# Four edits around the scan of a four-layer model: residual, softplus buffers, order of the state sums, and a shorter beginning

## The chip, the cores and the metric

The kernel runs on one core of a Trainium2 chip. The metric is the device time of one execution in microseconds (us), lower is better. The engines are named as in the profile: PE (TensorE, the matmuls; PEld are its weight loads), DVE (VectorE), ACT (ScalarE), POOL (GpSimd) and SP (SyncE, here a queue of DMAs). Each engine runs its own list of instructions in order, and waits where an instruction needs something that another engine or a DMA has not finished. Everything is float32.

## The reference, cut to what matters

The model takes `x` of 32 sequences, 256 positions each, 128 features. It has four layers of two halves. In front of each half there is a layer norm whose scale and shift depend on the sequence, and behind it a residual with a gate that depends on the sequence too:

```
mod = silu(c) @ wmod                     # one set of six vectors per layer
sa, ca, ga, sb, cb, gb = mod[:, 0..5]
ga, gb = (2*(g>=0) - 1) * max(|g|, 0.25) # for each of the two gates
h = layernorm(x) * (1 + ca) + sa
x = x + ga * attn(h)
h = layernorm(x) * (1 + cb) + sb
x = x + gb * ffn(h)
```

The change touches the setting up of `mod`, the reading of `x`, and the first half of the first layer, a selective scan (two branches, each with a softplus for `u` and one for `delta`):

```
xn    = layernorm(h);  xp = xn @ proj.T + b;  z = silu(xp)
u     = softplus(xp @ conv_br.T + b_br)
delta = softplus((u @ dbc[:, :64].T) @ dt.T + dt_b);  B, C = u @ dbc[:, 64:].T
state[t] = exp(delta[t] * A) * state[t-1] + delta[t] * B[t] * u[t]     # 16 states per feature
y_br[t]  = sum_n C[t, n] * state[t, n] + D * u[t]
out   = (y_0 + y_1) * z + h
```

The other seven halves (two mixtures of experts with capacity or dense, two attentions of other kinds, a linear attention, a mixture by heads and an MLP with FP4 rounding) are the same before and after.

## The kernel before, in words

The tokens are kept in SBUF for the whole kernel as 16 tiles `x[b]` of 128 features by 512 tokens (two sequences each). `run` calls `begin` and then the eight halves one after the other; each opens its own pools of buffers, so a half begins when the buffers of the one before are free.

**The beginning** (`begin`, L602 to L634). One DMA on ACT's queue brings `cT` and `wmod` of all four layers (`mw`, 1600 KB). For each layer there is a sigmoid (`sigmoid`, L552 to L556), six matmuls of 128 by 32, and some twenty tiny operations on DVE and ACT. For each of the 16 tiles there is a DMA of 256 KB (`xin`, three buffers, ACT's and SP's queue in turn), four transpositions on PE, and a copy to `x[b]`, on DVE or ACT in turn.

**The scan** (`scan_layer`). The work is written out as an agenda of steps: `put(t, f)` records that `f` is issued in step `t`, and within a step in the order of the calls. Tile `b` starts at step T = 16 b. The pair p = 8 b + 4 br + g takes two steps, `scan_even` in 2p and `scan_odd` in 2p + 1; one pair is four of the sixteen states of one branch:

- `scan_even`: 16 matmuls fill `dB` (four PSUM banks, one buffer), then DVE runs four scans `hs<-decay,dB` (L849) that read it. Then `scan_turned`: PE transposes half of the `hs` of the pair before into `hT` (one buffer of two banks), ACT copies it to `hsT0`. Then `scan_decay`: ACT makes two `decay` arrays for the next pair. Then `scan_weigh`: eight matmuls add the half `hsT1` of p - 2 into the state sums `y` (one PSUM bank, one buffer).
- `scan_odd`: `scan_turned` for the other half (`hsT1`), `scan_weigh` of `hsT0` of p - 1, `scan_decay`.

Between these lie the parts that prepare the tiles to come, and they all share a single PSUM bank, `tp` (the transposition bank): the two layer norms (steps T - 44 to T - 32), `scan_proj` (T - 21), the gate (T - 20, T - 19), `scan_u` and `scan_u2` (softplus of u, T - 19 and T - 18; T - 13 and T - 12 for the second branch), `scan_delta` and `scan_rows` (softplus of delta and the rows B and C, T - 15 and T - 14; T - 7 and T - 6), `scan_turn`, `scan_b`, `scan_c`. Behind the last pair of a tile ACT copies the sums (`scan_sum`, `yT`, T + 18), PE turns them back (`scan_end`, T + 21), DVE adds `uu` (L908), POOL multiplies by `z` and adds `h` (L914, L915), and in T + 23 DVE adds the residual into `x[b]` (L533).

A softplus is in two parts: `soft_start` (DVE, L739 and L740: `sp_r` = max(v + bias, 0), `sp_m` = v - 2 `sp_r`; one buffer each) and `soft_end` (ACT: exp and log on `sp_m`; POOL, L746: the sum of `sp_m` and `sp_r` into `u` or `dl`).

**What sets the order.** PE's matmuls and ACT's activations in the scan go through `mm`, `tr` and `act` (L386, L390, L393), which keep them in the order of the program. DVE's and POOL's instructions here don't: where they stand in their engine's list is decided when the kernel is built, by a planner that orders instructions by its own idea of when each could run.

Of the kernel before, what the change touches and what calls it, by code (L numbers as in the profile page):

```python
# [25 lines left out]
ALU = mybir.AluOpType  # L26
# [4 lines left out]
P = 128  # L31
NSEQ, SEQ = 32, 256
NB = 16
# [142 lines left out]
def packs(d):  # L176

    out = {}
# [3 lines left out]
        return g  # L182

    k = Pack()
    k.add("cT", np.stack([np.asarray(d[f"L{n}_c"]).T for n in range(4)], 1))
    k.add("wmod", np.stack([np.asarray(d[f"L{n}_wmod"]) for n in range(4)], 1))
    out["mod"] = k

    g, k = layer(0, "attn"), Pack()
# [120 lines left out]
class Program:  # L310
# [289 lines left out]


    def begin(self):  # L602
        nc, tc = self.nc, self.tc
        nc.scalar.preload_act_table_set(LN_EXP)
        with ExitStack() as ctx:
            self.pools(ctx, {"tp": 4, "mod": 2}, xin=3, mw=1)
            mw = self.wk("mw", (P, self.at["mod"]["n"]))
            nc.scalar.dma_start(mw, self.aps["mod"])
            v = View(mw, self.at["mod"]["at"])
            for n in range(4):  # L610
                sg = self.wk("sg", (P, NSEQ))
                self.sigmoid(sg, v.cT[:, n, :])
                nc.vector.tensor_tensor(sg, sg, v.cT[:, n, :], ALU.mult)
                ps = self.ps("mod", (P, 6, NSEQ))
                for j in range(6):
                    nc.tensor.matmul(ps[:, j, :], v.wmod[:, n, j * P : (j + 1) * P], sg, start=True, stop=True)
                m = self.mods[:, n]
                for j in (0, 3):
                    nc.scalar.copy(m[:, j, :], ps[:, j, :])
                    nc.vector.tensor_scalar(m[:, j + 1, :], ps[:, j + 1, :], 1.0, None, ALU.add)  # L620
                    neg, mag = self.wk("neg", (P, NSEQ)), self.wk("mag", (P, NSEQ))
                    nc.vector.tensor_scalar(neg, ps[:, j + 2, :], -1.0, None, ALU.mult)
                    nc.vector.tensor_tensor(mag, ps[:, j + 2, :], neg, ALU.max)
                    nc.vector.tensor_scalar(mag, mag, 0.25, 2.0, ALU.max, ALU.mult)
                    nc.vector.tensor_scalar(neg, ps[:, j + 2, :], 0.0, 0.5, ALU.is_ge, ALU.subtract)
                    nc.vector.tensor_tensor(m[:, j + 2, :], neg, mag, ALU.mult)
            xd = self.aps["x"].rearrange("(b t p) f -> b p t f", p=P, t=4)
            for b in range(NB):
                xi = self.wk("xin", (P, 4, P))
                (nc.sync if b % 2 else nc.scalar).dma_start(xi, xd[b])  # L630
                ps = self.ps("tp", (P, 4, P))
                for t in range(4):
                    nc.tensor.transpose(ps[:, t, :], xi[:, t, :], self.c.ident)
                (nc.scalar.copy if b % 2 else nc.vector.tensor_copy)(self.x[b], ps.rearrange("p a b -> p (a b)"))  # L634


    def scan_layer(self, w):

        nc = self.nc
        with ExitStack() as ctx:
            self.pools(
                ctx, {"dB": 1, "hT": 1, "y": 1, "tp": 1},
                h=4, z=3, dl=3, duT=3, bc=3, xn=1, ln_xn=1, xp=1, y=1, yT=1, rows=1, Xc=1, du=1, sg=1, hsT0=1, hsT1=1, sp_m=1, sp_r=1, Xr=1,
            )
# [8 lines left out]
            nc.scalar.copy(wd, pw[:, :P])  # L658
            decay = []
            for n in range(10):  # L660
                t = self.wk_pool.tile([P, 2, SEQ], F, name=f"decay{n}", bufs=1)
                nc.gpsimd.memset(t[:, :, 0:1], 0.0)
                decay.append(t)
            far = ctx.enter_context(self.tc.tile_pool(name="far", bufs=2, space=DRAM))
            s = {"far": far, "w": w, "A": A, "wd": wd, "decay": decay, "p": {}}
            agenda = {}

            def put(t, f, *args):
                agenda.setdefault(t, []).append((f, args))

            for p in range(-1, 8 * NB + 3):
                put(2 * p, self.scan_even, s, p)
                put(2 * p + 1, self.scan_odd, s, p)
            for b in range(NB):
                a = s[b] = {"b": b}
                T = 16 * b
                put(T, self.clear_regions)


                for o, n, src in ((T - 44, 1, lambda a: self.x[a["b"]]), (T - 36, 2, lambda a: a["h"])):  # L680
                    put(o, lambda a, n=n, src=src: a.update({("st", n): self.norm_rows(src(a), self.nc.gpsimd)}), a)
                    put(o + 1, lambda a, n=n: self.scan_roots(a, n), a)
                    put(o + 3, lambda a, n=n: self.norm_scale(a["st", n][0], *a["r", n]), a)
                put(T - 40, self.scan_norm_out, a)
                put(T - 32, self.scan_norm_out2, s, a)
                put(T - 21, self.scan_proj, s, a)
                put(T - 20, self.scan_gate, s, a)
                put(T - 19, self.scan_gate2, s, a)
                for br in (0, 1):
                    o = T + 8 * br  # L690
                    put(T - 19 + 6 * br, self.scan_u, s, a, br)
                    put(T - 18 + 6 * br, self.scan_u2, s, a, br)
                    put(o - 15, self.scan_delta, s, a, br)
                    put(o - 14, self.scan_rows, s, a, br)
                    put(o - 10, self.scan_turn, s, a, br)
                    put(o - 9, self.scan_b, s, a, br)
                    put(o - 5, self.scan_c, s, a, br)
                put(T + 18, self.scan_sum, s, a)
                put(T + 21, self.scan_end, s, a)
                put(T + 23, lambda a: self.residual(0, 0, a["b"], a["y"]), a)  # L700
            for t in sorted(agenda):
                for f, args in agenda[t]:
                    f(*args)
            self.strict = self.strict_act = False

    def scan_roots(self, a, n):
# [26 lines left out]
        self.act(a["z"], a["sg"], AF.Exp)  # L733
        self.nc.gpsimd.tensor_tensor(a["z"], a["z"], a["xp"], ALU.mult)

    def soft_start(self, src, bias):

        m, r = self.wk("sp_m"), self.wk("sp_r")
        self.nc.vector.tensor_scalar(r, src, bias, 0.0, ALU.add, ALU.max)  # L739
        self.nc.vector.scalar_tensor_tensor(m, r, -2.0, src, ALU.mult, ALU.add)  # L740
        return m, r, bias

    def soft_end(self, out, m, r, bias):
        self.act(m, m, AF.Exp, bias=bias)
        self.act(m, m, AF.Ln, bias=1.0)
        self.nc.gpsimd.tensor_tensor(out, m, r, ALU.add)  # L746

    def scan_u(self, s, a, br):
        w = s["w"]
        pu = self.ps("tp")  # L750
        self.mm(pu, w.conv[:, br, :], a["xp"])
        a["soft"] = self.soft_start(pu, w.vec[:, 3 + br : 4 + br])

    def scan_u2(self, s, a, br):
        a["u", br] = self.wk("u")
        self.soft_end(a["u", br], *a["soft"])

    def scan_delta(self, s, a, br):
        pt = self.ps("tp")
        self.mm(pt, s["wd"], a["u", br])  # L760
        a["soft"] = self.soft_start(pt, s["w"].vec[:, 5:6])

    def by_chunk(self, t):

# [2 lines left out]
    def scan_rows(self, s, a, br):  # L767
# [13 lines left out]
        dl = a["dl", br] = self.wk("dl")  # L781
        self.soft_end(dl, *a["soft"])
# [47 lines left out]
    def scan_even(self, s, p):  # L830
# [18 lines left out]
                nc.vector.tensor_tensor_scan(hs[:, :, n], decay, dB[:, :, n], 0.0, ALU.mult, ALU.add)  # L849
        self.scan_turned(s, p - 1, 0)  # L850
        self.scan_decay(s, p + 1, 0)
        self.scan_weigh(s, p - 2, 1)

    def scan_odd(self, s, p):
        self.scan_turned(s, p - 1, 1)
        self.scan_weigh(s, p - 1, 0)
        self.scan_decay(s, p + 1, 1)

    def scan_decay(self, s, p, half):
# [19 lines left out]
    def scan_weigh(self, s, p, h):  # L879
# [1920 lines left out]
```

## Time and profile before

| | us |
|---|---|
| runs | 6774.54, 6795.66, 6796.21; median 6795.66 |
| profiled execution | 6771.9, of which the span is 6769.9 |
| beginning, up to the first matmul of the scan layer | 0 to 43.65 |
| first layer's filling, up to the first `dB` | 43.65 to 125.1 |
| scans | 127.5 to 1100 |
| last residual of the scan | 1107.9 |
| the other seven halves | to 6769.9 |

A line of the timeline gives the start, the duration, the engine, the line of the source, the operation, what it writes and reads, the shape, and how many like it are merged; in brackets stands how long the engine was idle before and what ended that. In the table by stretches each engine has its busy time in that stretch with the number of its instructions; PEclk is the share of full speed that PE's clock was granted. Matmuls of a group overlap, so that the start of the next group is a better mark than the end that is shown. An instruction may be counted in several records (eight matmuls of `y` are 16 records).

### The profile page before, as it was taken

To read this page: it belongs to the slowest core of one execution; us is meant where nothing else is said; L and a number is where in the kernel's file an instruction comes from. 1 tells how busy PE (TensorE), PEld (TensorE's weight loads), DVE (VectorE), ACT (ScalarE), POOL (GpSimd) and SP (SyncE) were. 2 spreads that over 40 slices of the span, in tenths; PEclk is the share of its full clock that TensorE was granted. 3 is DMA by queue.
4 is the path that set the end of the run, shared out by engine and by line. 5 is a ranking of instruction groups with operands and counts; after the bars stand their busy time and mean duration, and the time that the engine had idled before them with its cause. 6 is when DMAs were issued, how large, how long until landed. Compare 5 with 4: busy or idle time off the path is not lost. (4 is left out here: it accounts for less than half of the span.)

```text
span 6769.9 us, 132928 instructions
## 1 busy us (share of the span) xinstructions
PE 5927.9 (88%) x54369; PEld 3341.0 (49%) x54369; DVE 4278.6 (63%) x9929; ACT 3493.9 (52%) x5035; POOL 2650.5 (39%) x2882
## 2 busy tenths in 40 slices
PE   5888886999899999999999767999889998999987
PEld 3555554466455555555566434555422222444444
DVE  3777776611455555555565644777777775677779
ACT  4888884333344444444444322443468886545542
POOL 3555553565444444444444443434234543000000
PEclk6999997999899999999999877888989998999998
DMA  1110111144000000000000101111134442000010
GB/s 60 41 41 29 41 41 35 42 124 119 15 6 5 5 8 5 5 8 5 5 2 2 47 17 26 26 24 26 31 79 90 92 91 49 16 18 18 18 33 30
DMA packets 175445, 232.19 MB, mean 34 GB/s; under 512 B 46519, under 2 KB 95919, under 8 KB 174450
## 3 DMA queue, kind: packets, MB, share of 16 engines
q1 hardware_dynamic: 120656, 124.40, 7.2%
q0 software_dynamic: 26992, 56.62, 3.5%
q10 hardware_dynamic: 27186, 42.67, 1.7%
q8 instruction: 426, 6.98, 0.4%
q14 instruction: 185, 1.52, 0.1%
HBM read 88.22 MB, written 74.97 MB: 24 GB/s over the span
## 5 line engine op out<-in xcount | busy, mean ns | idle before, releaser
L1418 ACT ACTIVATE E<-S 128x1024 f32<-128x1024 f32 x448 | 458.6, 1024 | 602.6 <-PE S L386 535.5
L298 DVE TENSOR_REDUCE mt<-S 128x4 f32<-128x1024 f32 (+1 forms) x512 | 549.8, 1087 | 252.5 <-PE S L386 196.1
L849 DVE TENSOR_TENSOR_SCAN hs<-decay,dB 128x512 f32<-128x512 f32 x512 | 583.0, 1204 | 91.8 <-PE dB L386 77.2
L386 PE MATMUL S<-qa,kx 32*128 32x256 f32 x4096 | 566.8, 396 | 59.8 <-DVE mt L298 39.0
L393 ACT ACTIVATE hid<-S,bigw 128x1024 f32<-128x1024 f32 x512 | 537.2, 1111 | 122.6 <-PE S L386 121.9
L1887 DVE TENSOR_TENSOR E<-S,cst 128x1024 f32<-128x1024 f32 x320 | 391.2, 1223 | 307.3 <-PE S L386 270.7
L1890 POOL TENSOR_SCALAR_AFFINE_SELECT E<-E 128x1024 f32<-128x1024 f32 x320 | 349.3, 1092 | 588.2 <-ACT E L1889 587.9
L386 PE MATMUL S<-kx,q 32*128 32x512 f32 (+1 forms) x2048 | 549.1, 631 | 16.9 <-ACT kx L1536 16.1
L1889 ACT COPY E<-S 128x1024 f32<-128x1024 f32 x320 | 323.5, 1011 | 328.4 <-PE S L386 244.7
L2439 POOL TENSOR_TENSOR acc<-acc,ye 128x512 f32<-128x512 f32 x256 | 344.5, 1346 | 362.7 <-DVE ye L298 319.6
L386 PEld LDWEIGHTS S<-qa,kx 32*128 32x128 f32 x4096 | 360.2, 200 | 178.4 <-DVE mt L298 107.1
L1719 DVE TENSOR_REDUCE mt<-S 128x4 f32<-128x512 f32 (+1 forms) x256 | 205.2, 823 | 320.9 <-PE S L386 312.4
L386 PE MATMUL S<-qG,f 32*128 32x512 f32 x2560 | 382.6, 658 | 4.5 <-DVE E L1887 3.4
L386 PE MATMUL S<-hm,bigw 32*128 32x512 f32 x2048 | 337.3, 650 | 24.8 <-ACT hid L393 24.8
L393 ACT ACTIVATE hsT<-hT 128x1024 f32<-128x1024 f32 x256 | 260.7, 1018 | 157.3 <-PE hT L390 156.2
L393 ACT ACTIVATE decay<-dl,A 128x510 f32<-128x510 f32 x512 | 339.1, 714 | 0.0
L386 PE MATMUL po<-E,vzl 128*32 128x128 f32 x8192 | 286.8, 281 | 59.6 <-POOL E L1890 59.3
L390 PE MATMUL hT<-cst,hs 128*128 128x128 f32 x2048 | 295.9, 290 | 22.6 <-ACT hsT L393 21.4
L386 PE MATMUL po<-hid,bigw 128*32 128x512 f32 x2048 | 279.9, 619 | 31.0 <-DVE ye L298 31.0
L386 PE MATMUL po<-E,vz 128*32 128x256 f32 x4096 | 304.7, 383 | 0.3 <-ACT oc L1438 0.2
L1422 POOL TENSOR_SCALAR_AFFINE_SELECT E<-E 128x512 f32<-128x512 f32 (+1 forms) x192 | 157.7, 822 | 364.4 <-ACT E L1418 363.9
L1766 ACT ACTIVATE E<-S 128x768 f32<-128x768 f32 (+1 forms) x192 | 168.9, 880 | 239.4 <-PE S L386 239.4
(524 smaller groups left out, 13192.1 us busy)
## 6 DMA issues: line engine op xcount, KB each, us to landing
gb<-gT SPq DMA_DIRECT2D x256, 256.0 KB
regions<-zeros ACTq DMA_DIRECT2D x16, 2048.0 KB
rx<-far SPq DMA_DIRECT2D x64, 256.0 KB
expert_rows<-eo SPq DMA_DIRECT2D x39, 256.0 KB
out<-out SPq DMA_DIRECT2D x16, 256.0 KB
xTd<-xT SPq DMA_DIRECT2D x15, 256.0 KB
xT<-xTd SPq DMA_DIRECT2D x15, 256.0 KB
bigw<-in_s SPq DMA_DIRECT2D x10, 256.0 KB
```

Of the source, the lines that this page charges most:

```text
L298: return lambda *args, **kw: self.tc.keep_in_program_order(op(*args, **kw))
L386: return self.tc.keep_in_program_order(self.nc.tensor.matmul(out, lhsT, rhs, start=start, stop=stop, **kw))
L390: return self.tc.keep_in_program_order(self.nc.tensor.transpose(out, in_, self.c.ident[:k, :k]))
L393: ins = self.nc.scalar.activation(*args, **kw)
L849: nc.vector.tensor_tensor_scan(hs[:, :, n], decay, dB[:, :, n], 0.0, ALU.mult, ALU.add)
L1418: nc.scalar.activation(e, src, AF.Exp, scale=scale)
L1719: nc.vector.tensor_reduce(m.rearrange("p (g j) -> p g j", j=2), pm[:, :, x] if i == 0 else pm[:, :, :, 0:192], AX.X, ALU.max, negate=True,)
L1766: nc.scalar.activation(e, src, AF.Exp, scale=1.0 / math.sqrt(8))
L1887: nc.vector.tensor_tensor(e, src, self.c.caus.unsqueeze(1).to_broadcast([P, 8, P]), ALU.mult)
L1889: nc.scalar.copy(e, src)
L1890: nc.gpsimd.affine_select(e, e, [[0, 8], [1, P]], ALU.is_ge, 0.0, base=0, channel_multiplier=-1)
L2439: nc.gpsimd.tensor_tensor(a["acc"], a["acc"], ye, ALU.add)
```

## The change

1. **Beginning.** `begin` now sets up `mod` for layer 0 alone and reads tile 0 alone. The host packs `c` and `wmod` of a layer side by side, so that a layer is one DMA of 400 KB. The other 15 tiles are read and turned in the agenda of the scan: tile b is loaded in step 2b - 47 and turned in step 2b - 45 (into the bank `dB`, which is idle until step 0), all loads on SP's queue with two buffers, all copies on DVE. The layers 1 to 3 of `mod` are loaded in step 8n - 52 and computed in step 8n - 46 (into the bank `y`). These matmuls and transpositions now go through `mm` and `tr`, so that they have a fixed place in PE's list.
2. **State sums.** `scan_weigh` is taken out of `scan_even` and `scan_odd`, and called at the end of the step, behind everything else that the step issues. `scan_sum` follows the last `scan_weigh` of a tile at once, which puts it behind the other parts of step T + 18.
3. **Softplus.** `soft_start` writes its first result straight into `u` or `dl`, and `soft_end` adds in place; `sp_r` is gone, `sp_m` has two buffers instead of one.
4. **Residual.** It is issued in step T + 25 instead of T + 23.

```diff
-            self.pools(ctx, {"tp": 4, "mod": 2}, xin=3, mw=1)
-            mw = self.wk("mw", (P, self.at["mod"]["n"]))
-            nc.scalar.dma_start(mw, self.aps["mod"])
...
+            self.pools(ctx, {"tp": 4, "mod": 2}, xin=3, mw=2)
+            for n in (0,) if some else range(4):
+                self.mod_layer(n, self.mod_load(n), self.ps("mod", (P, 6, NSEQ)))
+            for b in (0,) if some else range(NB):
+                self.turn_in(b, self.load_in(b), self.ps("tp", (P, 4, P)))
+    def mod_load(self, n):
+        mw = self.wk("mw", (P, NSEQ + 6 * P))
+        self.nc.scalar.dma_start(mw, self.aps["mod"][:, n * (NSEQ + 6 * P) : (n + 1) * (NSEQ + 6 * P)])
+        return mw
+    def mod_layer(self, n, mw, ps):
...
+        for j in range(6):
+            self.mm(ps[:, j, :], mw[:, NSEQ + j * P : NSEQ + (j + 1) * P], sg)
...
+    def load_in(self, b):
+        xi = self.wk("xin", (P, 4, P))
+        self.nc.sync.dma_start(xi, self.aps["x"].rearrange("(b t p) f -> b p t f", p=P, t=4)[b])
+        return xi
+    def turn_in(self, b, xi, ps):
+        for t in range(4):
+            self.tr(ps[:, t, :], xi[:, t, :])
+        self.nc.vector.tensor_copy(self.x[b], ps.rearrange("p a b -> p (a b)"))

     def scan_layer(self, w):
...
+            for b in range(1, NB):
+                put(2 * b - 47, lambda b=b: s.update({("xi", b): self.load_in(b)}))
+                put(2 * b - 45, lambda b=b: self.turn_in(b, s["xi", b], self.ps("dB", (P, 4, P))))
+            for n in (1, 2, 3):
+                put(8 * n - 52, lambda n=n: s.update({("mw", n): self.mod_load(n)}))
+                put(8 * n - 46, lambda n=n: self.mod_layer(n, s["mw", n], self.ps("y", (P, 6, NSEQ))))
+            sums = {}
             for p in range(-1, 8 * NB + 3):
...
+                sums[2 * p], sums[2 * p + 1] = (p - 2, 1), (p - 1, 0)
...
-                put(T + 18, self.scan_sum, s, a)
                 put(T + 21, self.scan_end, s, a)
-                put(T + 23, lambda a: self.residual(0, 0, a["b"], a["y"]), a)
+                put(T + 25, lambda a: self.residual(0, 0, a["b"], a["y"]), a)
             for t in sorted(agenda):
                 for f, args in agenda[t]:
                     f(*args)
+                if t in sums:
+                    self.scan_weigh(s, *sums[t])
...
-    def soft_start(self, src, bias):
-        m, r = self.wk("sp_m"), self.wk("sp_r")
-        self.nc.vector.tensor_scalar(r, src, bias, 0.0, ALU.add, ALU.max)
-        self.nc.vector.scalar_tensor_tensor(m, r, -2.0, src, ALU.mult, ALU.add)
-        return m, r, bias
+    def soft_start(self, out, src, bias):
+        m = self.wk("sp_m")
+        self.nc.vector.tensor_scalar(out, src, bias, 0.0, ALU.add, ALU.max)
+        self.nc.vector.scalar_tensor_tensor(m, out, -2.0, src, ALU.mult, ALU.add)
+        return out, m, bias
...
-        self.nc.gpsimd.tensor_tensor(out, m, r, ALU.add)
+        self.nc.gpsimd.tensor_tensor(out, m, out, ALU.add)
...
     def scan_even(self, s, p):
...
         self.scan_decay(s, p + 1, 0)
-        self.scan_weigh(s, p - 2, 1)
     def scan_odd(self, s, p):
         self.scan_turned(s, p - 1, 1)
-        self.scan_weigh(s, p - 1, 0)
         self.scan_decay(s, p + 1, 1)
...
     def scan_weigh(self, s, p, h):
...
+        if p % 8 == 7 and h == 1:
+            self.scan_sum(s, a)
```

More of the change, by code (lines that the diff above doesn't have):

```diff
@@ L184, in packs @@
     k = Pack()
-    k.add("cT", np.stack([np.asarray(d[f"L{n}_c"]).T for n in range(4)], 1))
-    k.add("wmod", np.stack([np.asarray(d[f"L{n}_wmod"]) for n in range(4)], 1))
+    k.add("mod", np.stack([np.concatenate([np.asarray(d[f"L{n}_c"]).T, np.asarray(d[f"L{n}_wmod"])], 1) for n in range(4)], 1))
     out["mod"] = k
@@ L602, in begin @@
     def begin(self):
-        nc, tc = self.nc, self.tc
-        nc.scalar.preload_act_table_set(LN_EXP)
+        self.nc.scalar.preload_act_table_set(LN_EXP)
+        some = 0 in self.stages
         with ExitStack() as ctx:
-            self.pools(ctx, {"tp": 4, "mod": 2}, xin=3, mw=1)
-            mw = self.wk("mw", (P, self.at["mod"]["n"]))
-            nc.scalar.dma_start(mw, self.aps["mod"])
[L609 to L634, printed above, removed]
@@ new lines, in mod_layer @@
+    def mod_layer(self, n, mw, ps):
+        nc = self.nc
+        sg = self.wk("msg", (P, NSEQ))
+        self.sigmoid(sg, mw[:, :NSEQ])
+        nc.vector.tensor_tensor(sg, sg, mw[:, :NSEQ], ALU.mult)
+        for j in range(6):
+            self.mm(ps[:, j, :], mw[:, NSEQ + j * P : NSEQ + (j + 1) * P], sg)
+        m = self.mods[:, n]
+        for j in (0, 3):
+            nc.scalar.copy(m[:, j, :], ps[:, j, :])
+            nc.vector.tensor_scalar(m[:, j + 1, :], ps[:, j + 1, :], 1.0, None, ALU.add)
+            neg, mag = self.wk("neg", (P, NSEQ)), self.wk("mag", (P, NSEQ))
+            nc.vector.tensor_scalar(neg, ps[:, j + 2, :], -1.0, None, ALU.mult)
+            nc.vector.tensor_tensor(mag, ps[:, j + 2, :], neg, ALU.max)
+            nc.vector.tensor_scalar(mag, mag, 0.25, 2.0, ALU.max, ALU.mult)
+            nc.vector.tensor_scalar(neg, ps[:, j + 2, :], 0.0, 0.5, ALU.is_ge, ALU.subtract)
+            nc.vector.tensor_tensor(m[:, j + 2, :], neg, mag, ALU.mult)
@@ L647, in scan_layer @@
                 ctx, {"dB": 1, "hT": 1, "y": 1, "tp": 1},
-                h=4, z=3, dl=3, duT=3, bc=3, xn=1, ln_xn=1, xp=1, y=1, yT=1, rows=1, Xc=1, du=1, sg=1, hsT0=1, hsT1=1, sp_m=1, sp_r=1, Xr=1,
+                h=4, z=3, dl=3, duT=3, bc=3, xn=1, ln_xn=1, xp=1, y=1, yT=1, rows=1, Xc=1, du=1, sg=1, hsT0=1, hsT1=1, Xr=1, mw=1,
             )
@@ L734, in scan_gate2, with soft_end @@
         self.nc.gpsimd.tensor_tensor(a["z"], a["z"], a["xp"], ALU.mult)
-    def soft_start(self, src, bias):
-        m, r = self.wk("sp_m"), self.wk("sp_r")
-        self.nc.vector.tensor_scalar(r, src, bias, 0.0, ALU.add, ALU.max)
-        self.nc.vector.scalar_tensor_tensor(m, r, -2.0, src, ALU.mult, ALU.add)
-        return m, r, bias
-    def soft_end(self, out, m, r, bias):
+    def soft_start(self, out, src, bias):
[3 more added lines that the diff above has]
+        return out, m, bias
+    def soft_end(self, out, m, bias):
         self.act(m, m, AF.Exp, bias=bias)
         self.act(m, m, AF.Ln, bias=1.0)
-        self.nc.gpsimd.tensor_tensor(out, m, r, ALU.add)
+        self.nc.gpsimd.tensor_tensor(out, m, out, ALU.add)
     def scan_u(self, s, a, br):
@@ L751, in scan_u @@
         self.mm(pu, w.conv[:, br, :], a["xp"])
-        a["soft"] = self.soft_start(pu, w.vec[:, 3 + br : 4 + br])
+        a["u", br] = self.wk("u")
+        a["soft"] = self.soft_start(a["u", br], pu, w.vec[:, 3 + br : 4 + br])
     def scan_u2(self, s, a, br):
-        a["u", br] = self.wk("u")
-        self.soft_end(a["u", br], *a["soft"])
+        self.soft_end(*a["soft"])
     def scan_delta(self, s, a, br):
@@ L760, in scan_delta @@
         self.mm(pt, s["wd"], a["u", br])
-        a["soft"] = self.soft_start(pt, s["w"].vec[:, 5:6])
+        a["dl", br] = self.wk("dl")
+        a["soft"] = self.soft_start(a["dl", br], pt, s["w"].vec[:, 5:6])
     def by_chunk(self, t):
@@ L780, in scan_rows @@
         nc.gpsimd.tensor_copy(a["Xc"].rearrange("k g r n -> k g n r"), Xc.rearrange("k (g n) r -> k g n r", g=4))
-        dl = a["dl", br] = self.wk("dl")
-        self.soft_end(dl, *a["soft"])
+        dl = a["dl", br]
+        self.soft_end(*a["soft"])
         a["du"] = self.wk("du", (P, 4, 4, 32))
```

## The prediction

> **What bounds the kernel now.** I read the page first (no engine is full, PE 88%, DVE 63%), then the table by stretches, then the timelines of one tile on each engine; the chain that ended last only covers the last thousand microseconds, so it says nothing here. The change touches the first 1108 us. In the table by stretches the filling (43 to 125 us) and the scans (125 to 1100 us) look like this:
>
> ```profile
> 43.00:125.00 82.00, 37.70 (x86) 15.21 (x86) 15.48 (x61) 35.16 (x75) 31.97 (x72) 0.50 0.01 2
> 125.00:1100.00 975.00, 791.25 (x11043) 562.84 (x11042) 726.50 (x897) 795.42 (x1286) 534.44 (x624) 0.94 0.11 40
> ```
>
> In both no engine is full (PE 791 and ACT 795 of 975 us): the time is in chains from engine to engine. The timeline of the beginning:
>
> ```profile
> 9.46 0.29 DVE L552 SCALAR_TENSOR_TENSOR sg_a<-mw 128x32 f32<-128x32 f32 x2 [9.46 <-DMA mw<-in_mod]
> ...
> 20.75 1.09 PE L633 MATMUL tp<-cst,xin 128*128 128x128 f32 x4 [1.24 <-DMA xin<-in_x]
> ...
> 44.80 1.11 PE L390 MATMUL tp<-cst,x 128*128 128x128 f32 x4 [0.36 <-ACT wd L658]
> ```
>
> The beginning waits for transfers; the first layer norm starts at 44.80. The load that PE waits for at 20.75 was issued at 17.69, so a tile's load takes 3 us. DVE in one tile of the scan:
>
> ```profile
> 573.07 0.75 DVE L739 TENSOR_SCALAR sp_r<-tp,w 128x512 f32<-128x512 f32 x1 [2.17 <-POOL dl L746]
> ...
> 580.03 0.65 DVE L908 TENSOR_TENSOR y<-uu,tp 128x512 f32<-128x512 f32 x1
> 584.53 1.32 DVE L533 SCALAR_TENSOR_TENSOR x<-y,mods,x 128x256 f32<-128x256 f32 x2 [3.85 <-POOL y L915]
> 585.77 4.54 DVE L849 TENSOR_TENSOR_SCAN hs<-decay,dB 128x512 f32<-128x512 f32 x4
> 592.60 4.55 DVE L849 TENSOR_TENSOR_SCAN hs<-decay,dB 128x512 f32<-128x512 f32 x4 [2.28 <-PE dB L386]
> ```
>
> A tile takes 62.04 us (585.77 to 647.81, the same four scans of the next tile). Two waits per tile belong to the edits: 3.85 us of the residual for POOL, 2.17 us of `sp_r` for POOL. PE in two places of the same tile, and ACT in the second:
>
> ```profile
> 602.95 0.64 PE L386 MATMUL y<-hsT,Cd 128*32 128x128 f32 x16
> 603.52 1.13 PE L386 MATMUL tp<-xn,w 128*128 128x512 f32 x2
> 604.58 1.17 PE L386 MATMUL dB<-Bd,duT 32*128 32x128 f32 x32
> ...
> 631.96 0.64 PE L386 MATMUL y<-hsT,Cd 128*32 128x128 f32 x16 [0.44 <-ACT yT L393]
> 632.53 1.12 PE L386 MATMUL tp<-xp,w 128*128 128x512 f32 x2
> 633.59 1.17 PE L386 MATMUL dB<-Bd,duT 32*128 32x128 f32 x32
> ```
>
> ```profile
> 631.32 0.58 ACT L393 ACTIVATE yT<-y 128x512 f32<-128x512 f32 x1
> 631.80 0.57 ACT L393 ACTIVATE rows<-tp 32x512 f32<-32x512 f32 x1
> 632.28 0.70 ACT L393 ACTIVATE sp_m<-sp_m,w 128x512 f32<-128x512 f32 x1
> 633.01 0.63 ACT L393 ACTIVATE sp_m<-sp_m 128x512 f32<-128x512 f32 x1
> ```
>
> What to see: `dB` to scan is 1.31 us at least (604.58 to 605.89), a scan group 4.55, and in five of the eight pairs of a tile `dB` starts when PE gets to it, not when DVE frees its bank (598.39, 604.58, 612.86, 626.88, 633.59). There PE comes from a user of `tp`, which had waited for ACT to empty that bank; the eight `y` matmuls (0.57 us) ran during that waiting.
>
> **The residual: 0.** The built program has another order than the agenda suggests. In its list for DVE the residual still stands behind `y<-uu,tp` and ahead of the next four scans, in all 16 tiles: the planner moved it back. So the 3.85 us stay. Had it gone behind the scans, a tile would win at most the wait and its own 1.3 us less what PE needs for `dB`, about 4 us.
>
> **Beginning: -31.6.** By the table in stretches of 2 us, the DMAs had moved 0.66 MB at 4 us, 1.46 at 6, 2.38 at 8. The new beginning needs `mw` of one layer (0.41 MB, alone on ACT's queue) and constants, weights and tile 0 (1.6 MB). By equal shares the bytes of `mw` are through at 4.4 us, those of tile 0 at 7.2. A load of 256 KB takes 3 us, of which 0.6 are bytes at 460 GB/s (the stretch 6 to 8 us); I add half of the rest, 1.2: 5.6 and 8.4. From `mw` (9.46) to the first `mod` matmul (15.7) before, less 3 us in which DVE stood at a copy of `x`, gives 8.7 now; six matmuls and some 15 tiny operations end near 12 us. The scan's pool waits for them, on all queues: the next loads on SP, and `tp<-w` on PE. So the first layer norm starts at about 13.2 instead of 44.80. Bounds: 11 (no wait for the pool) and 16 (transfers as slow as in 20 to 43 us, 127 GB/s, behind the first).
>
> **Filling: +11.7.** What left the beginning is now in PE's list between the steps of the norms: 15 tiles of four transpositions (1.09 us each, the row of 20.75) and 18 small matmuls (six in 1.3 us: twelve took 2.60 to 2.74). Where PE sat idle for 5 us (three `ln_xn`, ACT and POOL at work) two tiles fit in for nothing. In the gaps of about 1 us they don't: two tiles and a layer of `mod` (3.5) stand ahead of `tp<-h`, ahead of the second tile's `tp<-x` and ahead of `proj`, each +2.4 to 2.6; two single tiles +0.4 and +0.2. To this come 2.1 us where ACT has to do the sigmoid of layer 1 before `ln_t`, and that sigmoid waits for the load of `mw` and tile 1 (issued at 12, there at 15 or 16), and 0.8 twice, where eight tiny DVE operations (0.1 us apart) stand between the four `ln_st`. Sum 11.7. With two buffers a load starts when PE has turned the tile two before; by the walk it is there 1 to 5 us ahead of its place. On SP all 15 loads stand ahead of the first `far` (90.46), with nothing else between; the three `mw` loads on ACT's queue wait for nothing late; the 15 copies (0.69) lie in DVE's idle 66 of 82 us. Bounds: 4 (all hidden but the sigmoid and one `mod`) and 22 (15 tiles and three `mod` end to end, 20.3, and the sigmoid).
>
> The Trainium skill ("TensorE: Matmul & The Clock Gate", the HAM clock gate) has PE at half clock until about 3.4 us of sustained work. The row above has 0.50 for the whole filling with PE busy 46% of it. By the page the added work could reach full clock if it closed the gaps; then four transpositions would cost 0.66 as at 574.67, and the filling some 5 us less.
>
> **Softplus and state sums: +1.35 per tile.** I walk one tile in the new order of PE and ACT, with the durations above; scans start before at 592.60, 599.88, 605.89, 614.43, 620.34, 628.38, 636.56 and 647.81. `y` now stands behind the user of `tp`, right ahead of `dB`. ACT's lists are unchanged but for `yT`, so a user of `tp` isn't freed earlier. First pair: no change (PE idle 4.28 before it). Second: `tp<-u,wd` at 597.36 (behind ACT's `h`), `y` 598.39, `dB` 598.96 instead of 598.39, scans 600.27 (+0.39; they waited for `sp_m` before). Third: the pair of hand-overs starts 0.57 late, `tp<-xn,w` again behind ACT's `rows`, `dB` 605.65, scans 606.96 (+1.07). Fourth: ACT was busy without a gap here, so its delay stays 0.57; `dB` 614.00, scans 615.31 (+0.88, `sg` and `sp_m` in between had slack). Fifth: scans end 619.86, but `y` ends at 620.3; scans 621.61 (+1.27). Sixth: ACT's `xn` is 1.2 late, `y` 0.57: `dB` 628.65, scans 629.96 (+1.58). Seventh: the old wait of 2.17 is gone, as `sp_m` has a second buffer and `u` was last read by POOL in the tile before; but `yT` now stands behind `rows` and two `sp_m` on ACT, ends at 635.4 and holds back the first `y` of the next tile, and `dB` behind it: 636.05 instead of 633.59, scans 637.36 (+0.80). Eighth: ACT's `ln_xn` ends 642.3, `tp<-yT` 642.4, DVE's `y` 643.4, residual 647.93, scans 649.16 instead of 647.81: +1.35. So the softplus wins (alone it would give 1.1: the end of the wait moves the scans by 1.46, and ACT's `ln_xn` then sets the rest) and the sums lose more. Bounds per tile: -1.1 (`y` hidden everywhere) and +2.9 (five times 0.57, nothing won). Some 14 tiles have this pattern; the last two have little on `tp`. 14 x 1.35 = +19. The cover: POOL (534 of 975 us busy) delivers `dl` and `du` 2.7 us later, as its `Cd` waits for the last `y`; PE needs `du` 8 us on, so this costs nothing unless POOL falls behind by that.
>
> **Sum.** -31.6 + 11.7 + 19 = -1, against the profiled execution 6771.9. The median of the runs is 6795.66, 24 above it; I carry the change over to the median: 6795. The runs of before lie 22 us apart, about 0.3%, which is also what a measurement can tell from no change.
>
> **The rivals.** Faster, by hidden sums: if ACT's chain and not PE's order sets the five `dB`, as ACT's 82% would allow, a tile gives -1.1 and the sum is -20 - 15 = -35: 6761. Against it: each of the five `dB` follows a matmul within 0.05 us. Faster still: the residual does move in time because POOL's `y` is early; -4 x 14 more, 6740. Against: the order of the list, and POOL's three operations of 1.27 us behind DVE's `y` are unchanged. Slower, by the wait for `yT`: PE now stands still for ACT with `dB` behind it. From 2.5 us per tile on it outweighs the beginning by over 0.3% if the filling also takes its upper half: 14 x 2.9 = 41, less 31.6, plus 16: +25, 6821. For it: `y` waited 0.44 for `yT` even before. Last, the moved work is no gain at all (filling 22), with the tile as walked: +9, still no change that can be told.
>
> **How the numbers follow.** Chances: forecast (within 20 us) 0.45; hidden sums 0.27; residual moved 0.03; `yT` and sums at full price 0.25. The beginning and filling together span -30 to -7, the tiles -15 to +41: ends -45 and +34. The range is -43 to +32, which leaves out about one or two in ten: 6752 to 6827; the forecast's own is 6775 to 6815. Faster 0.30, same 0.45, slower 0.25.
>
> **What would show it.** First `tp<-cst,x` of the scan near 13 us, first `dB` near 105 instead of 125.1; the residual still idle about 3.85 us for POOL behind `y`; no DVE wait for POOL at `u<-tp,w`; a tile of 63.4 us; PE waiting for `yT` ahead of a `dB` 2.5 us later in the tile. I would be wrong if the tile takes 61 us or less, or if the filling stays as long as before.

## The result, and the profile after

| | before | after |
|---|---|---|
| median of 12 runs each, one chip, us | 6792.84 (6774.54 to 6797.32) | 6793.61 (6765.09 to 6802.03) |
| ratio | | 0.9999, 95% interval 0.9986 to 1.0012 |
| profiled execution, us | 6771.9 | 6801.5 |
| first layer norm of the scan, us | 44.80 | 14.95 |
| first scan | 127.52 | 109.24 |
| mean tile | 62.42 | 63.57 |
| start of the last residual of the scan | 1107.86 | 1108.38 |

The change makes no difference: what the beginning wins is lost again, almost to the microsecond, by the time the scan ends. The mean tile is from a group of four scans to the same group of the next tile, over the second to the thirteenth tile. The 30 us between the two profiled executions lie behind 1108 us, in halves whose instructions are the same.

The table by stretches of the kernel after (busy us and instructions of PE, PEld, DVE, ACT and POOL, then the granted clock, DMA share and GB/s):

```profile
43.00:125.00 82.00, 52.49 (x256) 28.31 (x256) 33.02 (x85) 41.12 (x83) 40.53 (x59) 0.67 0.16 52
125.00:1100.00 975.00, 778.81 (x10891) 562.57 (x10888) 720.70 (x885) 779.95 (x1264) 523.84 (x613) 0.94 0.10 37
```

PE is busier in the first stretch, since the last turnings of tiles, one layer of `mod` and the first scans now lie within it. The second stretch holds less of PE's work (10891 records against 11043), and the scans still end no earlier: they run slower. (The 0.67 is too high; the last section says why.) The beginning, PE's timeline after:

```profile
8.30 2.77 PE L385 MATMUL mod<-msg,mw 128*128 128x32 f32 x12 [8.30 <-DVE msg L623]
10.88 1.09 PE L389 MATMUL tp<-cst,xin 128*128 128x128 f32 x4
13.84 0.76 PE L385 MATMUL tp<-w 64*128 64x128 f32 x2 [1.86 <-DVE mods L635]
14.95 1.11 PE L389 MATMUL tp<-cst,x 128*128 128x128 f32 x4 [0.36 <-ACT wd L670]
```

One layer of `mod` and one tile stand ahead of the first layer norm; then the scan's pool waits for the last tiny operation of `mod` (`DVE mods`). DVE in one tile after:

```profile
572.76 0.67 DVE L934 TENSOR_TENSOR y<-uu,tp 128x512 f32<-128x512 f32 x1
577.27 1.32 DVE L532 SCALAR_TENSOR_TENSOR x<-y,mods,x 128x256 f32<-128x256 f32 x2 [3.84 <-POOL y L941]
578.51 4.54 DVE L875 TENSOR_TENSOR_SCAN hs<-decay,dB 128x512 f32<-128x512 f32 x4
...
627.99 0.75 DVE L764 TENSOR_SCALAR u<-tp,w 128x512 f32<-128x512 f32 x1 [0.43 <-PE tp L385]
628.85 0.69 DVE L765 SCALAR_TENSOR_TENSOR sp_m<-u,tp 128x512 f32<-128x512 f32 x1
630.40 4.55 DVE L875 TENSOR_TENSOR_SCAN hs<-decay,dB 128x512 f32<-128x512 f32 x4 [0.86 <-PE dB L385]
```

The residual still stands right behind `y<-uu,tp` and waits 3.84 us for POOL. The softplus (`u`) no longer waits for POOL (before: 2.17 us at `sp_r`), but the scans behind it wait for `dB`. Why, PE and ACT show at the same place:

```profile
626.76 1.12 PE L385 MATMUL tp<-xp,w 128*128 128x512 f32 x2 [0.43 <-ACT rows L392]
628.51 0.65 PE L385 MATMUL y<-hsT,Cd 128*32 128x128 f32 x16 [0.63 <-ACT yT L392]
629.09 1.17 PE L385 MATMUL dB<-Bd,duT 32*128 32x128 f32 x32
```

```profile
626.13 0.57 ACT L392 ACTIVATE rows<-tp 32x512 f32<-32x512 f32 x1
626.61 0.70 ACT L392 ACTIVATE sp_m<-sp_m,w 128x512 f32<-128x512 f32 x1
627.35 0.63 ACT L392 ACTIVATE sp_m<-sp_m 128x512 f32<-128x512 f32 x1
627.88 0.58 ACT L392 ACTIVATE yT<-y 128x512 f32<-128x512 f32 x1
```

`y` now stands between the user of `tp` and `dB`, and `yT` behind `rows` and two `sp_m`; here `y` waits 0.63 us for `yT` on top. On the page, DVE's idle time ahead of the scans for PE's `dB` grew from 77.2 to 120.9 us (before, then after; behind the busy time and the mean stands the idle time, and then the share of it that `dB` ended):

```profile
L849 DVE TENSOR_TENSOR_SCAN hs<-decay,dB 128x512 f32<-128x512 f32 x512 | 583.0, 1204 | 91.8 <-PE dB L386 77.2
L875 DVE TENSOR_TENSOR_SCAN hs<-decay,dB 128x512 f32<-128x512 f32 x512 | 583.0, 1203 | 132.2 <-PE dB L385 120.9
```

### The profile page after: what moved, and what is told of

Read it like the earlier page. It is cut to its first block, busy times and chain, and to the rows that moved or that the text cites. A ratio compares the mean times of both kernels' runs of the same rounds, so it can differ in the third digit from the quotient of the medians.

```text
span 6799.6 us, 132890 instructions
## 1 busy us (share of the span) xinstructions
PE 5941.4 (87%) x54369; PEld 3361.6 (49%) x54369; DVE 4297.2 (63%) x9937; ACT 3489.0 (51%) x5026; POOL 2656.7 (39%) x2882
## 5 line engine op out<-in xcount | busy, mean ns | idle before, releaser
L875 DVE TENSOR_TENSOR_SCAN hs<-decay,dB 128x512 f32<-128x512 f32 x512 | 583.0, 1203 | 132.2 <-PE dB L385 120.9
L389 PE MATMUL hT<-cst,hs 128*128 128x128 f32 x2048 | 297.5, 291 | 18.7 <-ACT hsT L392 13.3
```

The costliest lines, as they stand in the source:

```text
L389: return self.tc.keep_in_program_order(self.nc.tensor.transpose(out, in_, self.c.ident[:k, :k]))
```

## The experiments

They ran on two other chips, on which before takes 6687 to 6695 us. Single executions of one kernel lie up to 30 us apart, mostly behind the scan. So the marks of the scan in each trace tell the parts apart, and the ratio (against before on the same chip) is the check. In three rows (softplus alone, last sum in the old place, only even sums late) the ratio is 8 to 11 us from what the last residual says, a little outside its interval, so that behind the scan something differs there that no run explains. All of them:

| kernel | first scan | mean tile | last residual | ratio, 95% interval |
|---|---|---|---|---|
| beginning alone | 110.09 | 62.43 | 1089.19 | 0.9974, 0.9964 to 0.9983 |
| softplus alone | 126.67 | 61.32 | 1093.24 | 0.9990, 0.9980 to 0.9999 |
| late sums alone | 129.21 | 64.97 | 1146.34 | 1.0056, 1.0034 to 1.0078 |
| after, last sum of a tile in the old place | 109.20 | 63.36 | 1105.52 | 1.0013, 1.0002 to 1.0023 |
| after, only sums of odd steps late | 110.24 | 64.71 | 1123.95 | 1.0026, 1.0015 to 1.0037 |
| after, only sums of even steps late | 109.88 | 64.47 | 1118.75 | 1.0002, 0.9992 to 1.0011 |
| after, all sums in the old place | 110.16 | 61.38 | 1077.58 | 0.9955, 0.9943 to 0.9967 |
| after, residual really later, T + 23 | 110.09 | 58.97 | 1036.51 | 0.9901, 0.9879 to 0.9923 |
| the same, T + 25 | 109.37 | 58.92 | 1036.26 | 0.9893, 0.9870 to 0.9916 |
| old sums and residual later, T + 23 | 109.34 | 55.94 | 995.79 | 0.9836, 0.9812 to 0.9860 |
| the same, mod layers 1 to 3 at the end | 104.35 | 55.93 | 1001.09 | 0.9840, 0.9825 to 0.9856 |
| after once more | 110.00 | 63.64 | 1110.07 | 1.0001, 0.9992 to 1.0010 |

**One part at a time, from the kernel before.** The residual's part alone (T + 25 for T + 23) was not run: in the trace of the kernel after, the residual stands at the same place of DVE's list as before in all 16 tiles. The other three have the edits of the diff above, each by itself.

The beginning:

```diff
+            for n in (0,) if some else range(4):
+                self.mod_layer(n, self.mod_load(n), self.ps("mod", (P, 6, NSEQ)))
+            for b in (0,) if some else range(NB):
+                self.turn_in(b, self.load_in(b), self.ps("tp", (P, 4, P)))
...
```

> The kernel before with the beginning alone changed (layer 0 and tile 0 first, the rest inside the filling). Theory: the parts of the change add up, and this one gives its full -18 us: the first layer norm near 15.0 us instead of 44.8, the first scan near 109.2 instead of 127.5, a tile of 62.0 us as before, the last residual of the scan near 1089.6 instead of 1107.9, the whole -18 us. Rival A: the time won at the front is given back inside the scan, because the loads, turnings and mod layers disturb the first tiles; then the last residual stands at 1100 or later, though the first scan is early. Rival B: it is the other parts that lengthen the filling; then the first scan comes near 98.

Measured: first scan 110.09, tile 62.43, last residual 18.7 us earlier, ratio 0.9974 (17 us). Nothing is given back later, and the filling is not lengthened by the other parts: both rivals fall.

The softplus:

```diff
-        m, r = self.wk("sp_m"), self.wk("sp_r")
-        self.nc.vector.tensor_scalar(r, src, bias, 0.0, ALU.add, ALU.max)
+        m = self.wk("sp_m")
+        self.nc.vector.tensor_scalar(out, src, bias, 0.0, ALU.add, ALU.max)
...
```

> The kernel before with the softplus alone changed (no sp_r, two buffers of sp_m). Theory: the 2.17 us for which DVE waits for POOL at sp_r go, PE and ACT then hold the rest back, and a tile takes 60.9 us instead of 62.04; the last residual 15 to 17 us earlier, the whole -16 us. Rival: what the wait hid takes its place in full (the next scans wait for PE or ACT instead), a tile of 62.0 and no change.

Measured: tile 61.32 (-1.10; the 60.9 expected came from a tile of 62.04, and the mean one of before is 62.42), last residual 14.6 us earlier. The ratio shows 1 to 13 us of it; where the rest went behind the scan is not shown. The 1.1 us that the prediction's walk gave the softplus, of the 2.17 us of waiting, hold.

The sums:

```diff
-        self.scan_weigh(s, p - 2, 1)
...
-        self.scan_weigh(s, p - 1, 0)
...
+                if t in sums:
+                    self.scan_weigh(s, *sums[t])
...
```

> The kernel before with the state sums alone put at the end of their step, and yT behind the last of them. Theory: five of eight groups of dB start 0.57 us or more later each; with the softplus worth -1.1 a tile and both together +1.62, the sums alone cost +2.7: a tile of 64.7 us, the last residual near 1146, the whole +38 us; DVE's idle time ahead of the scans for PE's dB grows from 92 us to over 120. Rival A (sums hidden behind ACT's chain): tile 62 to 62.4, at most +5. Rival B (only the wait for yT hurts): tile near 62.7, +10, and the second to sixth group of scans of a tile stand where they did.

Measured: tile 64.97 (+2.55), last residual +38.5, ratio +0.56% (37 us). In the kernel before, with the sums alone late, the page has for the scans:

```profile
L852 DVE TENSOR_TENSOR_SCAN hs<-decay,dB 128x512 f32<-128x512 f32 x512 | 582.9, 1203 | 119.1 <-PE dB L386 107.6
```

Idle time 119.1 us, 107.6 of it for `dB` (before 91.8 and 77.2): hidden sums are ruled out, and 64.97 is far over the 62.7 of a loss by `yT` alone.

**Which sums.** From the kernel after, some of the sums put back.

```diff
-                if t in sums:
+                if t in sums and not (sums[t][0] % 8 == 7 and sums[t][1]):
...
+        if (p - 2) % 8 == 7:
+            self.scan_weigh(s, p - 2, 1)
```

> The changed kernel, but the last state sum of each tile, with yT behind it, is back in its old place; the other fifteen stay at the end of their steps. Theory: the wait for yT costs little. It holds back the seventh group alone: tile 63.0 instead of 63.66, about -9 us against the changed kernel; the groups two to six unchanged (6.8, 14.8, 21.5, 29.8, 36.1, 44.5 us from the first). Rival: yT is the main loss of the sums: tile near 61, -38 us against the changed kernel.

Measured: 63.36, only 0.2 to 0.3 less than the 63.57 and 63.64 of the two profiles of the kernel after. The theory's 0.65 was too much; the rival is out by far. The wait for `yT` is a side matter here.

```diff
-                if t in sums:
+                if t in sums and sums[t][1] == 0:
...
+        self.scan_weigh(s, p - 2, 1)
```

> The changed kernel with the late place for the state sums of the odd steps alone; those of the even steps, with yT, are back in their old places. Theory: dB is issued first in an even step, so that the sums at the end of the odd step are what stands between a user of tp and dB: nearly the whole loss is here. A tile takes 63.2 to 63.5 us (63.68 with all sums late, 61.27 with all in the old place). Rival: it is the number of sums moved that counts, not the step: then half of the loss, near 62.4.

Measured: a mean of 64.71, more than with all sums late, which neither expected. The tiles are of two kinds: two of the twelve take 63.44 and 63.45, as the theory has it, the others 64.88 to 65.10. Order and waits are the same in both. PE, first in a long tile, then at the same place in a short one:

```profile
355.22 2.07 PE L385 MATMUL tp<-xp,w 128*128 128x512 f32 x2 [1.79 <-ACT ln_xn L392]
357.22 1.08 PE L385 MATMUL y<-hsT,Cd 128*32 128x128 f32 x16
358.23 1.36 PE L385 MATMUL dB<-Bd,duT 32*128 32x128 f32 x32
...
614.96 1.13 PE L385 MATMUL tp<-xp,w 128*128 128x512 f32 x2 [1.79 <-ACT ln_xn L392]
616.01 0.64 PE L385 MATMUL y<-hsT,Cd 128*32 128x128 f32 x16
616.59 1.17 PE L385 MATMUL dB<-Bd,duT 32*128 32x128 f32 x32
```

The granted clock in the two stretches (last but two in the line):

```profile
355.20:359.60 4.40, 4.38 (x51) 2.34 (x52) 2.71 (x11) 2.91 (x6) 1.85 (x4) 0.61 0.00 0
614.90:618.00 3.10, 3.04 (x53) 1.97 (x54) 2.83 (x12) 2.95 (x7) 0.59 (x2) 1.00 0.00 0
```

PE idles 1.79 us both times. In the long tile it comes back at half clock (2.07 for 1.13, 1.08 for 0.64), and `dB` starts 1.4 us later. In a tile without this drop of the clock the sums of the odd steps cost 63.44 - 61.38 = 2.1 us (61.38 is the mean tile with all sums in the old place): they carry the loss, as the theory had it.

```diff
-                if t in sums:
+                if t in sums and sums[t][1] == 1:
...
+        self.scan_weigh(s, p - 1, 0)
```

> The changed kernel with the late place for the state sums of the even steps alone, yT behind the last of them; those of the odd steps are back in their old places. Theory: behind an even step come other transpositions before the next dB, so these cost little: a tile of 61.3 to 61.7 us. Rival: half of the loss, near 62.4.

Measured: 64.47; both expectations are wrong. PE, in a tile of 64.86:

```profile
628.42 1.08 PE L385 MATMUL y<-hsT,Cd 128*32 128x128 f32 x16 [2.19 <-ACT yT L392]
629.43 2.08 PE L385 MATMUL tp<-xp,w 128*128 128x512 f32 x2
631.44 1.30 PE L385 MATMUL dB<-Bd,duT 32*128 32x128 f32 x32
```

With the sums of the odd steps early, the first `y` of the next tile stands ahead of `tp<-xp,w` again, while `yT` stays late. So the wait for `yT` is 2.19 us instead of 0.63, the user of `tp` stands behind it, and PE comes back at half clock. Whether `yT` is cheap or dear depends on where the next `y` is: moved apart, the even sums cost 3.1 us a tile in this run and the odd ones 3.3 in the one before, against 2.2 for both together. The other seven intervals between the groups of scans of a tile take on average what they take with all sums early, within 0.2 us: the sums of the even steps other than the last of a tile cost next to nothing.

**All sums back.** The old three calls in `scan_even`, `scan_odd` and step T + 18, the rest as after.

```diff
+        self.scan_weigh(s, p - 2, 1)
...
+        self.scan_weigh(s, p - 1, 0)
...
+                put(T + 18, self.scan_sum, s, a)
-                if t in sums:
-                    self.scan_weigh(s, *sums[t])
```

> The changed kernel with all state sums back in their old places: new beginning, new softplus, the agenda's later residual. Theory: the sums are the whole loss inside the scan; tile 60.9 us instead of 63.66, first scan near 109.2, last residual near 1074, the whole -33 us against the kernel before. Rival: the parts do not add up, because the sums and the softplus act on the same chain (the tile stays above 62): -18 us or less.

Measured: tile 61.38 (softplus alone 61.32), last residual 1077.58, ratio 0.9955 (30 us). The sums are the whole loss in the scan; without them beginning and softplus add up to within 3 us (18.7 + 14.6 against 30.3 at the last residual). The residual's later step is in this kernel too, and it changes nothing that can be seen: the tile is that of the softplus alone.

**The residual really later.** Scans and residual kept in the order of the program, so that the planner can't move them. (Shown for T + 23; the other run has `put(T + 25, self.scan_residual, a)`.)

```diff
-                nc.vector.tensor_tensor_scan(hs[:, :, n], decay, dB[:, :, n], 0.0, ALU.mult, ALU.add)
+                self.tc.keep_in_program_order(
+                    nc.vector.tensor_tensor_scan(hs[:, :, n], decay, dB[:, :, n], 0.0, ALU.mult, ALU.add)
+                )
...
-                put(T + 25, lambda a: self.residual(0, 0, a["b"], a["y"]), a)
+                put(T + 23, self.scan_residual, a)
...
+    def scan_residual(self, a):
+        self.nc.vector.on = True
+        self.residual(0, 0, a["b"], a["y"])
+        self.nc.vector.on = False
```

> The changed kernel, but DVE's scans and the residual are kept in the order of the program, and the residual is issued in step T + 23: on DVE it stands behind the four scans that followed it. All else is as in the changed kernel. Theory: the 3.85 us of waiting for POOL leave the path, and the scans start when PE's dB is there, 1.3 us after its start: some 4 us a tile less, tile 59.6, about -60 us against the changed kernel. The residual fits in the 2.3 us in which DVE waits for the next dB. Rival: ACT or PE had used the 3.85 us to catch up; then a tile wins 2 us or less, 30 us at most.

> As the one with the residual kept behind the scans, but issued in step T + 25, which is the agenda of the changed kernel taken at its word: on DVE it stands one group of scans later, right ahead of the softplus of the next delta. Theory: the same wait is gone, but here DVE does not idle for 2.3 us and the residual's 1.3 us delay sp_m for ACT: tile 60 to 60.6, 0.4 to 1 us more than in step T + 23. Rival: no difference between the two (under 0.2 us a tile), as the residual lies beside other work in both.

Measured: 58.97 and 58.92, that is -4.6 and -4.7 a tile, 72 to 74 us earlier at the last residual, ratios 0.9901 and 0.9893. The gain is larger than the wait of 3.85 us and than the 4 us expected, and the two steps don't differ: in T + 25 the residual lies in the time in which DVE waits for the user of `tp` of the next `dl`. Of the twelve tiles of each run six take 58.3 to 58.4 and six 59.4 to 59.6; the latter have one drop of the clock, the former none.

With the old sums as well:

> New beginning, new softplus, old state sums, and the residual kept behind the scans in step T + 23. Theory: everything that wins together: tile 60.9 - 4 = 56.9, first scan near 109.2, last residual near 1015, the whole -92 us against the kernel before. Rival: with the waits on POOL gone another engine sets the tile (ACT, busy 795 of 975 us before, or PE), and a tile does not go below 59: -60 us at most.

Measured: 55.88 to 55.95 in the second to the thirteenth tile, ratio 0.9836 (110 us; the medians, 6576.76 against 6695.24, differ by 118). It beats both kernels; the rival's floor of 59 is passed. DVE where the residual is:

```profile
523.46 0.66 DVE L938 TENSOR_TENSOR y<-uu,tp 128x512 f32<-128x512 f32 x1
524.24 4.56 DVE L873 TENSOR_TENSOR_SCAN hs<-decay,dB 128x512 f32<-128x512 f32 x4
528.71 0.85 DVE L297 SCALAR_TENSOR_TENSOR x<-y,mods,x 128x256 f32<-128x256 f32 x2
530.15 4.55 DVE L873 TENSOR_TENSOR_SCAN hs<-decay,dB 128x512 f32<-128x512 f32 x4 [0.59 <-ACT decay L392]
```

No wait of DVE for POOL is left between 170 and 920 us, and the scans behind wait 0.59 us instead of 2.28. The granted clock of the same 750 us, in the kernel after and, below, in this one:

```profile
170.00:920.00 750.00, 602.34 (x8206) 431.51 (x8204) 551.64 (x703) 606.34 (x1001) 422.51 (x506) 0.93 0.10 37
```

```profile
170.00:920.00 750.00, 657.75 (x9427) 454.86 (x9426) 620.13 (x789) 688.70 (x1126) 478.28 (x564) 1.00 0.12 43
```

By the clock records, 92 of the 750 us are at half clock before, 99 after, 82 with old sums, 21 with the residual later, none here. In the kernel after PE comes back from its own wait for the scans like this:

```profile
583.10 2.09 PE L385 MATMUL dB<-Bd,duT 32*128 32x128 f32 x32 [2.45 <-DVE hs L875]
585.13 1.97 PE L389 MATMUL hT<-cst,hs 128*128 128x128 f32 x8
```

2.09 instead of 1.17 and 1.97 instead of 1.09. With the sums put back the same `dB` takes 2.09 too, behind a wait of 5.13. In the kernel with old sums and the residual later it hardly waits:

```profile
528.85 1.17 PE L385 MATMUL dB<-Bd,duT 32*128 32x128 f32 x32 [0.17 <-DVE hs L873]
```

From the sums put back to the residual moved as well, the interval between two groups of scans that held the residual shrinks from 11.45 to 6.48 us, by the wait (3.85) and the residual's own time (1.1), which now lies in the wait for the next `dB`. The next one shrinks by 0.90, about as much as a `dB` at half clock takes more, and the one behind it grows by 0.42: 5.4 in all. So the gain beyond the wait is the residual's own time and the clock, as far as these intervals tell them apart.

**What the filling is made of.** On top of the last kernel:

```diff
-        self.nc.scalar.dma_start(mw, self.aps["mod"][:, n * (NSEQ + 6 * P) : (n + 1) * (NSEQ + 6 * P)])
+        (self.nc.sync if n else self.nc.scalar).dma_start(mw, self.aps["mod"][:, n * (NSEQ + 6 * P) : (n + 1) * (NSEQ + 6 * P)])
...
-                put(8 * n - 52, lambda n=n: s.update({("mw", n): self.mod_load(n)}))
-                put(8 * n - 46, lambda n=n: self.mod_layer(n, s["mw", n], self.ps("y", (P, 6, NSEQ))))
+                put(8 * n + 226, lambda n=n: s.update({("mw", n): self.mod_load(n)}))
+                put(8 * n + 233, lambda n=n: self.mod_layer(n, s["mw", n], self.ps("tp", (P, 6, NSEQ))))
```

> The fastest so far (new beginning, new softplus, old sums, residual kept behind the scans), with the layers 1 to 3 of mod taken out of the filling and put between the last scans, in the transposition bank, their loads on SP's queue. It tests how the cost of the filling is made up. Theory, by the prediction's terms: 2.1 us for the sigmoid, 1.6 for the tiny operations on DVE and 1.2 to 1.3 of each of the three gaps go: the first scan 7 to 8 us earlier, near 102 instead of 109.3 (in the trace of the page, where the first norm starts near 15). At the end each layer costs 1 to 3 us, as DVE and PE wait for the sigmoid there: the whole between -5 and +2. Rival: the tiles' turnings alone make the 11.6 us; then the first scan stays at 107 or later.

Measured: first scan at 104.35, 5.0 earlier: by their removal, the three mod layers make 5.0 of the 11.6 us, not 7 to 8, and the turnings and the rest 6.6; both the theory's 102 and the rival's 107 are missed. From first scan to last residual it takes 10.3 us more, 3.4 for each layer, so that the last residual comes 5.3 later and the whole is not better. In the filling they were cheaper.

**The changed kernel once more.**

> The changed kernel once more, on the chip of these runs. By the marks in the scan (the last residual at the same place as before, +0.6 us) the ratio is 1.000, within 0.15%. The 30 us by which the first two profiled executions differ behind the scan come and go between executions: its profile then has the later halves elsewhere again. Rival: the change does something to the later halves; then they are longer by some 20 to 30 us than those of the kernel before on this chip, and the ratio is near 1.003 to 1.004.

Measured: 1.0001, 0.9992 to 1.0010. From the end of its last residual to the end of the span it takes 5581 us; the eleven other experiments, whose later halves are the same, take 5563 to 5588. So single executions differ by 25 us there, and with the medians of before and after 0.8 us apart on the first chip, the 30 us between the first two profiles are not shown to be an effect of the change.

## Why the prediction was right

The sum (-1, at the last residual +0.5) and the mechanism are right: the beginning's gain is lost in the filling and to sums that stand on the path from a user of `tp` to `dB`. That it comes out within 2 us is partly luck, since two of the three totals, the filling and the scans, are met with parts that were not the ones worked out. The first layer norm came at 14.95 (13.2 forecast), the first `dB` at 106.83 (105).

- **Residual, 0**: right, by the order of the list (in 15 tiles; behind the last one no scans follow). What it would be worth "had it moved" was put at about 4 us a tile, and that is too small: 4.6 to 5.4. The bound took about 1.2 us off again for PE's `dB`, but behind `y<-uu,tp` the scans wait only 0.70 us for it in a tile without a drop of the clock (at 310.03, T + 23), and 0.1 with old sums. It also took PE's durations as they stood; those behind the wait were half-clock durations, which go with it.
- **Beginning, -31.6**: measured -29.85. The first `mod` matmul came at 8.30 (worked out: 8.7), but the tiny operations behind it ended at 13.8, not at 12; DVE's copy of tile 0 (0.68 us at 12.06) stood between them.
- **Filling, +11.7**: measured 94.29 - 82.72 = +11.57. The total is right, its make-up not quite: the terms with `mod` in them come to 7.4 us, and taking `mod` out saved 5.0. The 5 us that the prediction had from the Trainium skill ("TensorE: Matmul & The Clock Gate", the HAM clock gate), if the gaps closed, did not come: PE worked without a gap from 24.1 to 31.8, from 36.3 to 44.0 and from 48.3 to 55.7, and only the last brought full clock, for 6.8 us. In other runs with this beginning the first full clock is recorded at 32.0 to 61.7 us, for 3.4 or 6.8 us each time, and the first scan comes at 109.2 to 110.2 all the same. Two turnings, at 57.6 and 59.9, take 0.60; the other thirteen take 1.06 to 1.12 as before.
- **Softplus and sums, +1.35 a tile**: the mean is +1.15, in the walked tile +1.62 (it is the shortest of the twelve before, 62.04 against a mean of 62.42); the 0.3 there come in the second pair, where PE was still at half clock (`hT` 1.97, `y` 1.08), for which the walk had no term. The parts are right apart: softplus -1.10 (walked -1.1), sums +2.55 alone (walked +2.45). The term of 19 us is met at 18.8, but in another way: twelve tiles give 13.8, the first tile 4.0, which was not walked, and the end 1.0. In the first tile PE waits 2.58 us for ACT instead of 0.94 and then runs at half clock.
- **The rivals**: hidden sums fall by the sums alone (+38.5, where they needed none); the full price of `yT` by its 0.2 to 0.3 us; no gain of the moved work by the beginning alone (-18.7). That the residual would move was ruled out by the list.

What the change would have been worth without the sums is 30 us, and with the residual kept behind the scans as well (measured in T + 23), 110.

## What to carry to other kernels

A step in an agenda is not a place in an engine's list: look at the built order first, and keep an instruction in order if its place is the point. Between a matmul that waits for another engine and one that a bound engine waits for, even 0.6 us of ready work is on the path; put it ahead of the first, where the waiting hides it. Price a wait of PE at more than its length: what follows it may run at half clock, and this comes and goes from tile to tile.

## What the runs showed of the hardware

- **Half clock after short waits.** PE dropped to half clock around idle times of 1.79, 2.19, 2.45 and 2.58 us; behind another of 2.36 us, in the first tile before, it did not (`dB` 1.17 at 147.89). The clock changes in steps of 3.41 us: the records of a drop within the scans last 3.4, 6.8 or, less often, 10.2 us, and the long and the short tile shown of the run with odd sums have the same order and waits and differ in whether it came. The same page of the Trainium skill has a free-running window of 3413 ns, which agrees; its rule that gaps of PE over about 3.4 us are to be avoided (HAM oscillation) is too lenient by this trace, since 1.79 us was enough in the one tile shown, and not in the other. What decides it is not shown.
- **The start of the clock record says nothing.** After, the record has its first entry at 56.5 us, and the table counts all before it as 1.00, which also lifts the 0.67 of the filling; four transpositions take 1.06 to 1.12 us there, and 0.60 at full clock.
- **Chips differ behind the scan only.** The scan takes the same on the two chips that ran the kernel after (last residual at 1108.4 and 1110.1), but the whole takes 6793.6 on one and 6690.2 on the other. The difference in the profiles is 108 us, 95 of it between 3670 and 5070 us, where the slower chip has more half clock (454 against 304 us in the same work). Why it has more stays open.
